# Moving a difference and a three-way split to GpSimd in a two-layer transformer kernel

## The chip, the cores and the metric

The kernel runs on one core of a Trainium2 chip. The metric is the device time of one execution in microseconds (us). Engines are named as in the profile: PE is the matrix engine, DVE is VectorE, ACT is ScalarE, POOL is GpSimd, and SP issues the DMAs. Each engine runs its own queue in order, and engines wait for each other by semaphores.

## The reference

Four sequences of 2048 tokens with 256 channels pass through two layers. Layer 0 is a causal attention with one head of 64 and a linear layer on fp8-rounded activations. Layer 1 is a causal attention with 16 heads of 16 and rotary positions, and a gated FFN that mixes each token with the one before it. Each of the four parts is added to its input behind a layer normalization without weights.

```python
x = x + attn0(layernorm(x))
x = x + ffn0(layernorm(x))
x = x + attn1(layernorm(x))
# FFN of layer 1, on h = layernorm(x); h_prev is h shifted by one token
xr = mu_r * h + (1.0 - mu_r) * h_prev
xk = mu_k * h + (1.0 - mu_k) * h_prev
x = x + sigmoid(xr @ W_r.T) * (square(relu(xk @ W_k.T)) @ W_v.T)
```

## The kernel before

**Tiles and stages.** The work goes in blocks of 512 tokens (`BLK`), 16 in all, ordered by sequence. Layer 1's attention is the main stream: for each block four groups of four heads, 64 groups in all, and for each group one step per 128 keys (4, 8, 12 or 16 steps, more for later blocks of a sequence). In a step PE computes the scores of four heads, transposed (`scores_of`, L799), ACT takes their exponential (L826), and PE weights the values with the exponentials of the step before (`weighted`, L841). In the same step PE computes scores for a later group, not transposed (`maxima_of`, L773), of which DVE only takes the maximum over the keys (L796). Four heads share PE by rows of 32.

**The maxima and their split.** When the last maximum of a group is taken, the function `end` inside `all_maxima` (L972) reduces them to one negative maximum per token and head, `nm` (L975, 128 partitions by 16 columns). `shift_pads` (L442) splits `nm` into three bfloat16 parts whose sum has its precision, by four small instructions (L445 to L448), each of which reads what the one before it wrote: the first part is `nm` rounded, `rest` is what is left, the second part is `rest` rounded, the third what is then left. The parts go into a zeroed tile `pad`. `shift_rows` (L450) has PE turn this tile (L455) and ACT copy the result into `sh` (L459). In the following group, matmuls of `ones` with `sh` add the shift to the scores. The call of `shift_of` (L1222) stands at the end of a group's last step, and `end` is called one step earlier for most groups. PE runs in order, so whatever stands behind L455 in its queue waits with it. Layer 0's attention (`a_mid`, L513) makes the same split for its one head, 16 times (L535).

**The side work and the order.** Everything else is written as generators: layer 0 (`a_in`, `a_mid`, `a_out`), the projections, rotation, keys and queries of layer 1 (`b_...`), and layer 1's output projection and FFN (`end_half`, L869, one for each half block of 256 tokens, 32 in all). They fill the gaps of the main stream. A planner decides while the program is written: the class `Clock` (L41) follows every instruction with a fixed price for each engine and form, and keeps when each buffer is written. A generator yields the PE work that its next piece takes, the number of buffers it needs, and the tiles it needs. The planner (`pull`, L1049) writes the piece when by its model these tiles are ready within 150 ns of PE's time. So a changed price or engine moves all later side work. The order in each engine's queue is that of writing.

**The mix.** In `end_half` the normalized tokens stand transposed in `xs_`, with one column more for the token before; `cur` is the view without that column. Small POOL copies (L889 to L893) fill the first column and keep the last one. For each of the two mixes and each half of the channels (128 on the partitions), ACT makes (1 - mu) * previous (L901), and DVE adds mu * current (L904). The factor 1 - mu is made once, in `prepare` (L315). The matmuls with `wk` (L914) and `wr` read the mixes.

Of the kernel before, what the change touches and what calls it, by code (L numbers as in the profile page):

```python
# [12 lines left out]
F32 = mybir.dt.float32  # L13
# [9 lines left out]
P = 128  # L23
# [167 lines left out]
def seq_kernel(  # L191
# [101 lines left out]
    wv = load_w(wvT, "wv", C)  # L293
    mu_sb = const.tile([P, 2, CK], F32, name="mu_sb")
    nc.sync.dma_start(mu_sb, mu)
    omu_sb = const.tile([P, 2, CK], F32, name="omu_sb")

    def prepare():

        wcf, wce, wcm = wfs
        nc.vector.tensor_scalar(wcf, wcf, 448.0, -448.0, ALU.min, ALU.max)
        nc.vector.tensor_scalar(
            wce.bitcast(I32), wcf.bitcast(I32), 0x7F800000, None, ALU.bitwise_and
        )
        nc.vector.tensor_scalar(wcm, wce, 2.0**-6, 1.5 * 2.0**20, ALU.max, ALU.mult)
        nc.vector.tensor_tensor(wcf, wcf, wcm, ALU.add)
        nc.vector.tensor_tensor(
            wf16.rearrange("p k n -> p (k n)"), wcf, wcm, ALU.subtract  # L310
        )
        nc.vector.tensor_scalar_mul(nsin_sb, sin_sb, -1.0)
        wv_flat = wv.rearrange("p k n -> p (k n)")
        nc.vector.tensor_scalar_mul(wv_flat, wv_flat, 0.5)
        nc.vector.tensor_scalar(omu_sb, mu_sb, -1.0, 1.0, ALU.mult, ALU.add)  # L315

# [57 lines left out]
    def w2t(name):  # L376
        return w2(name).rearrange("p (k n) -> p k n", k=CK)
# [61 lines left out]
        transpose(xn, out_to[0], f"{tag}_{hf}", nc.scalar.copy)  # L439
        done(1)  # L440

    def shift_pads(nm, pad, heads):  # L442
        part = [pad[:, :, :heads, i] for i in range(3)]
        rest = small.tile([P, TT, HG], F32, tag="rest", name="rest")[:, :, :heads]
        nc.vector.tensor_copy(part[0], nm)  # L445
        nc.vector.tensor_tensor(rest, nm, part[0], ALU.subtract)
        nc.vector.tensor_copy(part[1], rest)
        nc.vector.tensor_tensor(part[2], rest, part[1], ALU.subtract)  # L448

    def shift_rows(pad, sh, name):  # L450

# [61 lines left out]
    def a_mid(b, qb):  # L513
        tag = f"a0_{b}_{qb}"
        while (b, qb, "in", 0) not in flags or (b, qb, "in", 1) not in flags:
            yield None
        qh, ql = q0.pop((b, qb))[:2]

        mx = small.tile([P, TT, NB], F32, tag="mx0", name=f"mx_{tag}")
        for t in range(TT):  # L520
            for kb in range(qb + 1):
                yield 0.6, 0, qh, ql, kT0[kb]
                sc = bank(f"m_{tag}_{t}_{kb}")
                w = BLK if kb < qb else (t + 1) * P
                for q in (qh, ql):
                    nc.tensor.matmul(  # L526
                        sc[:, :w], q[:, t * P : (t + 1) * P], kT0[kb][:, :w],
                        start=(q is qh), stop=(kb < qb and q is ql),
                    )
                if kb == qb:  # L530
                    nc.tensor.matmul(sc[:, w - P : w], ident_b, mask_b, start=False, stop=True)
                nc.vector.reduce_max(mx[:, t, kb : kb + 1], sc[:, :w], axis=AX.X)  # L532
        nm = small.tile([P, TT], F32, tag="nm0", name=f"nm_{tag}")
        nc.vector.tensor_reduce(nm, mx[:, :, : qb + 1], AX.X, ALU.max, negate=True)
        shift_pads(nm[:, :, None], pads[2], 1)  # L535
        yield 0.3, 2, pads[2][:, :, 0, :3]
        sh = work.tile([P, BLK], BF16, tag="sh0", name=f"sh_{tag}", bufs=2)
        shift_rows(pads[2], sh, f"sh_{tag}")
        cx, sums = w2(f"cx_{tag}"), w2(f"sum_{tag}")

        nkt = (qb + 1) * TT
        pTs = []
        for kt in range(nkt):
            yield 0.9, 1, sh
            sc = bank(f"s_{tag}_{kt}")
            pT = w2(f"p_{tag}_{kt}")
            c0 = max(kt - qb * TT, 0) * P
            keys = kT0[kt // TT][:, (kt % TT) * P : (kt % TT + 1) * P]
            diag = kt >= qb * TT
            nc.tensor.matmul(sc[:, c0:], ones, sh[:, c0:], start=True, stop=False)  # L550
            nc.tensor.matmul(sc[:, c0:], keys, qh[:, c0:], start=False, stop=False)
            nc.tensor.matmul(sc[:, c0:], keys, ql[:, c0:], start=False, stop=not diag)
            if diag:
                nc.tensor.matmul(
                    sc[:, c0 : c0 + P], ident_b, maskT_b, start=False, stop=True
                )
            nc.scalar.activation(pT[:, c0:], sc[:, c0:], AF.Exp, scale=D0**-0.5)  # L557
            pTs.append(pT)
            if kt % 2:
                if diag:  # L560
                    c0 -= P
                    nc.gpsimd.memset(pT[:, c0 : c0 + P], 0.0)
                narrow.append((b, qb, kt - 1, c0, pTs, cx, sums))
                pTs = []
        done(2)
        while (b, qb, "ctx", nkt - 2) not in flags:
            yield None
        ctx0[b, qb] = cx, sums
# [300 lines left out]
    def end_half(b, qb, x, cn, hf):  # L869
        tag = f"f1_{b}_{qb}_{hf}"  # L870
        yield 0.6, 2, cn[:, 2 * hf : 2 * hf + 2, :]
        cT = w2t(f"cT_{tag}")
        transpose(cn[:, 2 * hf : 2 * hf + 2, :], cT, f"c{tag}", nc.scalar.copy)
        flags.add((b, qb, "cT", hf))
        yield 1.8, 0, cT
        po = bank(f"po_{tag}")
        for j in range(2):
            token_mm(po[:, j * C : (j + 1) * C], cT, wo1, j)
        done(1)
        xh = x[:, 2 * hf : 2 * hf + 2, :].rearrange("p t c -> p (t c)")  # L880
        nc.vector.tensor_tensor(xh, po, xh, ALU.add)

        xs_ = work.tile([P, CK, HALF + 1], F32, tag="xs", name=f"xs_{tag}", bufs=2)
        cur = xs_[:, :, 1:]
        yield from normal_T(x, [cur], hf, f"f1_{b}_{qb}")
        while hf and (b, qb, 0) not in edges:
            yield None
        if (qb, hf) == (0, 0):
            nc.gpsimd.memset(xs_[:, :, 0:1], 0.0)  # L889
        else:  # L890
            nc.gpsimd.tensor_copy(xs_[:, :, 0:1], edges.pop((b, qb - (1 - hf), 1 - hf)))
        edges[b, qb, hf] = small.tile([P, CK, 1], F32, tag="edge", name=f"edge_{tag}", bufs=3)
        nc.gpsimd.tensor_copy(edges[b, qb, hf], xs_[:, :, HALF : HALF + 1])  # L893
        while hf and (b, qb, "mid") not in flags:
            yield None
        yield 0.0, 3, xs_
        mix = []
        for i in (1, 0):
            m = w2t(f"mix_{tag}_{i}")
            for k in range(CK):  # L900
                nc.scalar.activation(  # L901
                    m[:, k, :], xs_[:, k, :HALF], AF.Copy, scale=omu_sb[:, i, k : k + 1]
                )
                nc.vector.scalar_tensor_tensor(  # L904
                    m[:, k, :], cur[:, k, :], mu_sb[:, i, k : k + 1], m[:, k, :],
                    ALU.mult, ALU.add,
                )
            mix.append(m)
        xk, xr = mix
        yield 1.8, 0, xk  # L910
        pk = bank(f"pk_{tag}")
        for d in range(CK):
            for k in range(CK):
                nc.tensor.matmul(  # L914
                    pk[:, d * HALF : (d + 1) * HALF], wk[:, k, d * P : (d + 1) * P],
                    xk[:, k, :], start=(k == 0), stop=(k == CK - 1),
                )
        done(1)
        ka = w2(f"ka_{tag}")
        nc.scalar.activation(ka, pk, AF.Relu)  # L920
        nc.gpsimd.tensor_tensor(ka, ka, ka, ALU.mult)
        flags.add((b, qb, "mid"))
        yield 1.8, 0, xr
        pr = bank(f"pr_{tag}")
        for j in range(2):
            token_mm(pr[:, j * C : (j + 1) * C], xr, wr, j)
        done(1)
        sg = w2(f"sg_{tag}")

        nc.scalar.activation(sg, pr, AF.Tanh, scale=0.5)  # L930
        yield 1.8, 0, ka
        po = bank(f"pw_{tag}")
        for j in range(2):
            token_mm(po[:, j * C : (j + 1) * C], ka.rearrange("p (k n) -> p k n", k=CK), wv, j)
        nc.vector.scalar_tensor_tensor(sg, sg, 1.0, po, ALU.add, ALU.mult)  # L935
        nc.gpsimd.tensor_tensor(xh, xh, sg, ALU.add)  # L936
        done(2)
        t0 = qb * BLK + hf * HALF
        nc.sync.dma_start(
            out[b, t0 : t0 + HALF, :].rearrange("(t p) c -> p t c", p=P),  # L940
            x[:, 2 * hf : 2 * hf + 2, :],
        )
        flags.add((b, qb, "end", hf))
# [16 lines left out]
    def all_maxima():  # L960


        for G, (i, b, qb, g) in enumerate(groups):
            n = steps[G]
            lead = steps[max(G - 1, 0)]
            for s in range(n):
# [5 lines left out]
                def end(G=G, s=s, n=n, mx=mx, qb=qb, b=b, g=g):  # L972
                    if s == n - 1:
# [1 line left out]
                        nc.vector.tensor_reduce(  # L975
                            nm, mx[:, :, :, : qb + 1], AX.X, ALU.max, negate=True
                        )
                        shift_pads(nm, pads[G % 2], HG)

                yield at_, i, (b, qb, g, s, mx), end  # L980

# [331 lines left out]
```

## Time and profile before

| | |
|---|---|
| time before, median of 3 runs | 3005.61 us (2993.38 to 3006.42) |
| profiled execution | 2996.61 us |
| its span | 2994.9 us |
| granted PE clock, mean | 0.97 |
| PE idle between matmuls in the span (2994.9 - 2813.5) | 181 us |
| L901, ACT's part of the mix | 128 instructions, mean 505 ns |
| L904, DVE's part of the mix | 128 instructions, mean 557 ns |
| L445 / L446 / L447 / L448, the split | 64 / 64 / 80 / 80 instructions (L447 and L448 with the 16 of layer 0), mean 267 / 228 / 229 / 232 ns |
| two-input POOL instructions, 256 and 512 columns (L692, L936) | mean 736 and 1294 ns |

The profile is that of one execution. Its first part gives each engine's busy time as a share of the span; its chain follows the work that ended last back through whatever released each step. A group of instructions is shown as line, engine, operation, tiles and count, then busy time, mean duration in ns, and the idle time of the engine just before them with what ended it. An engine that stands idle costs nothing unless the chain runs over it.

### The profile page before, as it was taken

Reading aid. Unit: us, or ns where it says so; the run is one execution under the profiler, and the core shown is the slowest. Engines: PE = TensorE matmul, PEld = TensorE weight load, DVE = VectorE, ACT = ScalarE, POOL = GpSimd, SP = SyncE. Lnnn points to the kernel's source line nnn. Section 1 sums busy time; section 2 is a strip of 40 time slices with the busy share of each in tenths; the row PEclk is TensorE's granted clock in tenths of the full one; section 3 lists DMA queues with packets and bytes.
Section 4 is the critical chain, followed back from the end, with each engine's and each line's share of the span. In section 5 each row is a group of like instructions: output and inputs, shape, how many; then the busy total and the mean of one; then the engine's idle time right before and its main releaser. Section 6 shows DMA issues by size and latency. Waiting matters only on the chain.

```text
span 2994.9 us, 68331 instructions
## 1 busy us (share of the span) xinstructions
PE 2813.5 (94%) x27616; PEld 1532.4 (51%) x27616; DVE 2095.7 (70%) x4536; ACT 1743.4 (58%) x3681; POOL 913.8 (31%) x1246
## 2 busy tenths in 40 slices
PE   6899999999999999999999999999999999999998
PEld 3555555555456555545455555554545655454444
DVE  4567767787566787887747677878765678678761
ACT  2445467566654656656665565666666555665664
POOL 4524344041232405313214342513122341340001
PEclk9889999999999999999999999999999999999999
DMA  2000000000000000000000000000000000000000
GB/s 89 1 12 5 22 2 5 23 1 26 4 9 15 5 22 5 22 2 5 23 12 5 12 16 12 5 23 2 26 2 12 16 5 15 2 8 2 5 2 11
DMA packets 28781, 36.70 MB, mean 12 GB/s; under 512 B 3312, under 2 KB 22064, under 8 KB 28464
## 3 DMA queue, kind: packets, MB, share of 16 engines
q1 hardware_dynamic: 28464, 32.32, 3.8%
q8 instruction: 217, 3.56, 0.5%
q14 instruction: 100, 0.82, 0.1%
HBM read 11.24 MB, written 8.39 MB: 7 GB/s over the span
## 4 chain that ended last, share of the span: by engine, by line
PE 74%; DVE 18%; ACT 3%; POOL 2%; issue 2%; DMA 1%; POOLq 0%; SPq 0%; DVEq 0%; ACTq 0%
PE av L844 16%; PE s L811 14%; PE m L781 13%; DVE mx L796 10%; PE pq_a L423 3%; PE pv_a L423 2%; PE pk_f L914 2%; PE av_a L580 2%; PE pr_f L423 2%; PE po_f L423 2%; PE pw_f L423 2%; ACT p L826 1%; DVE mx_a L532 1%; PE m L790 1%; PE s_a L550 1%
## 5 line engine op out<-in xcount | busy, mean ns | idle before, releaser
L796 DVE TENSOR_REDUCE mx<-m 128x1 f32<-128x512 f32 (+3 forms) x2560 | 1414.3, 602 | 524.8 <-PE m L781 222.6
L826 ACT ACTIVATE p<-s 128x512 f32<-128x512 f32 (+3 forms) x2560 | 1223.5, 533 | 852.9 <-PE s L811 467.7
L781 PE MATMUL m<-kT_a,qh_a 32*128 32x512 f32 (+3 forms) x2560 | 698.8, 463 | 66.2 <-DVE mx L796 47.2
L811 PE MATMUL s<-qh_a,kT_a 32*128 32x512 f32 (+3 forms) x2560 | 651.3, 502 | 8.0 <-ACT p L826 4.2
L844 PE MATMUL av<-p,v_a 128*32 128x512 f32 (+3 forms) x5120 | 644.0, 548 | 0.1
L781 PEld LDWEIGHTS m<-kT_a,qh_a 32*128 32x128 f32 x2560 | 297.9, 186 | 598.7 <-DVE mx L796 223.1
L781 PE MATMUL m<-kT_a,ql_a 32*128 32x512 f32 (+3 forms) x2560 | 535.8, 390 | 0.0
L811 PE MATMUL s<-sh,ones 32*128 32x512 bf16 (+3 forms) x2560 | 483.7, 356 | 18.2 <-ACT p L826 13.7
L811 PE MATMUL s<-ql_a,kT_a 32*128 32x512 f32 (+3 forms) x2560 | 482.7, 367 | 0.0
L781 PEld LDWEIGHTS m<-kT_a,ql_a 32*128 32x128 f32 x2560 | 261.0, 189 | 20.8 <-issue 19.5
L811 PEld LDWEIGHTS s<-qh_a,kT_a 32*128 32x128 f32 x2560 | 250.9, 189 | 33.3 <-ACT p L826 10.2
L811 PEld LDWEIGHTS s<-ql_a,kT_a 32*128 32x128 f32 x2560 | 250.0, 188 | 1.2
L811 PEld LDWEIGHTS <-ones 32*128 32x128 bf16 x2560 | 126.6, 91 | 184.7 <-issue 161.1
L844 PEld LDWEIGHTS av<-p,v_a 128*32 128x32 f32 x5120 | 112.0, 108 | 161.5 <-issue 117.0
L587 POOL TENSOR_TENSOR sum_a<-p_a,p_a 128x512 f32<-128x512 f32 x16 | 20.5, 1279 | 466.5 <-ACT p_a L557 441.6
L592 POOL TENSOR_TENSOR sum_a<-sum_a,p_a 128x512 f32<-128x512 f32 (+1 forms) x128 | 146.6, 1145 | 5.0
L819 PE MATMUL s<-mask_q,mask_k 32*128 32x128 bf16 (+1 forms) x2048 | 136.9, 208 | 0.0
L790 PE MATMUL m<-mask_k,mask_q 32*128 32x64 bf16 x2048 | 129.8, 197 | 0.0
L592 POOL TENSOR_TENSOR cx_a<-cx_a,avs_a 128x512 f32<-128x512 f32 (+1 forms) x64 | 73.1, 1143 | 180.3 <-ACT avs_a L590 180.3
L423 PE MATMUL pq_a<-wqkv,xT_a 128*128 128x512 f32 x256 | 123.5, 605 | 1.9 <-DVE mx L796 1.8
L936 POOL TENSOR_TENSOR x<-x,sg_f 128x512 f32<-128x512 f32 x32 | 41.4, 1294 | 271.4 <-DVE sg_f L935 271.4
L532 DVE TENSOR_REDUCE mx_a<-m_a 128x1 f32<-128x512 f32 (+3 forms) x160 | 87.5, 600 | 11.9 <-PE m_a L526 8.4
(163 smaller groups left out, 3991.2 us busy)
## 6 DMA issues: line engine op xcount, KB each, us to landing
x<-in_x SPq DMA_DIRECT2D x16, 512.0 KB, 4.0
out_y<-x SPq DMA_DIRECT2D x32, 256.0 KB, 2.1
qh_a<-th_a SPq DMA_DIRECT2D x32, 128.0 KB, 2.4
ql_a<-tl_a SPq DMA_DIRECT2D x32, 128.0 KB, 2.4
kT_a<-th_a SPq DMA_DIRECT2D x16, 128.0 KB, 2.4
kT_a<-tl_a SPq DMA_DIRECT2D x16, 128.0 KB, 2.4
wqkv<-in_wqkv1T SPq DMA_DIRECT2D x1, 768.0 KB, 8.6
wc<-in_wfT SPq DMA_DIRECT2D x1, 256.0 KB, 7.0
```

Of the source, the lines that this page charges most:

```text
L423: nc.tensor.matmul(dst, lhsT[:, k, t * P : (t + 1) * P], w[:, k, :], start=(k == 0), stop=(k == CK - 1),)
L532: nc.vector.reduce_max(mx[:, t, kb : kb + 1], sc[:, :w], axis=AX.X)
L580: nc.tensor.matmul(av[z * SLOT : (z + 1) * SLOT, c0:], v0[kt // TT][:, kt % TT + j, d * SLOT : (d + 1) * SLOT], pTs[j][:, c0:], start=True ...
L592: nc.gpsimd.tensor_tensor(to[:, c0:], to[:, c0:], add[:, c0:], ALU.add)
L781: nc.tensor.matmul(sc[:, :w], q1[b, qb, g // 2][i][r, g % 2, t * P : (t + 1) * P], kT1[b, kb][r, g, :w], start=(i == 0), stop=(kb < qb and ...
L790: nc.tensor.matmul(sc[:, w - P + lo : w - P // 2 + lo], mask_q[r, v, :], mask_k[r, v, lo : lo + P // 2], start=False, stop=(v == 1),)
L796: nc.vector.reduce_max(mx[:, t, h, kb : kb + 1], sc[:, :w], axis=AX.X)
L811: nc.tensor.matmul(sc[:, c0:], lhsT, rhs, start=(i == 0), stop=(i == 2 and not diag))
L819: nc.tensor.matmul(sc[:, c0 : c0 + hi], mask_k[r, v, :], mask_q[r, v, :hi], start=False, stop=(v == 1),)
L826: nc.scalar.activation(pTs[h][:, c0:], sc[:, c0:], AF.Exp, scale=DK**-0.5)
L844: nc.tensor.matmul(av[h * SLOT : (h + 1) * SLOT, c0:], v1[b, kt // TT][:, kt % TT, at : at + SLOT], pTs[h][:, c0:], start=(kt == 0), stop= ...
L914: nc.tensor.matmul(pk[:, d * HALF : (d + 1) * HALF], wk[:, k, d * P : (d + 1) * P], xk[:, k, :], start=(k == 0), stop=(k == CK - 1),)
```

## The change

The mix is written with one difference: previous + mu * (current - previous). POOL makes the difference once for each half block, DVE makes both mixes from it, and ACT has no part in it; the difference lies in the tile of the mix that is made last. The tile of 1 - mu is dropped. `shift_pads` takes the engine as an argument: POOL for the 64 groups of layer 1, DVE as before for layer 0.

```diff
-    omu_sb = const.tile([P, 2, CK], F32, name="omu_sb")
...
-        nc.vector.tensor_scalar(omu_sb, mu_sb, -1.0, 1.0, ALU.mult, ALU.add)
...
-    def shift_pads(nm, pad, heads):
+    def shift_pads(nm, pad, heads, engine):
         part = [pad[:, :, :heads, i] for i in range(3)]
         rest = small.tile([P, TT, HG], F32, tag="rest", name="rest")[:, :, :heads]
-        nc.vector.tensor_copy(part[0], nm)
-        nc.vector.tensor_tensor(rest, nm, part[0], ALU.subtract)
-        nc.vector.tensor_copy(part[1], rest)
-        nc.vector.tensor_tensor(part[2], rest, part[1], ALU.subtract)
+        engine.tensor_copy(part[0], nm)
+        engine.tensor_tensor(rest, nm, part[0], ALU.subtract)
+        engine.tensor_copy(part[1], rest)
+        engine.tensor_tensor(part[2], rest, part[1], ALU.subtract)
...
-        shift_pads(nm[:, :, None], pads[2], 1)
+        shift_pads(nm[:, :, None], pads[2], 1, nc.vector)
...
         yield 0.0, 3, xs_
-        mix = []
-        for i in (1, 0):
-            m = w2t(f"mix_{tag}_{i}")
+
+        mix = [w2t(f"mix_{tag}_{i}") for i in range(2)]
+        nc.gpsimd.tensor_tensor(mix[0], cur, xs_[:, :, :HALF], ALU.subtract)
+        yield 0.0, 0, mix[0]
+        for m, i in ((mix[1], 1), (mix[0], 0)):
             for k in range(CK):
-                nc.scalar.activation(
-                    m[:, k, :], xs_[:, k, :HALF], AF.Copy, scale=omu_sb[:, i, k : k + 1]
-                )
                 nc.vector.scalar_tensor_tensor(
-                    m[:, k, :], cur[:, k, :], mu_sb[:, i, k : k + 1], m[:, k, :],
+                    m[:, k, :], mix[0][:, k, :], mu_sb[:, i, k : k + 1], xs_[:, k, :HALF],
                     ALU.mult, ALU.add,
                 )
-            mix.append(m)
-        xk, xr = mix
+        xr, xk = mix
         yield 1.8, 0, xk
...
-                        shift_pads(nm, pads[G % 2], HG)
+                        shift_pads(nm, pads[G % 2], HG, nc.gpsimd)
```

## The prediction

> **What bounds the kernel now.** I read the page first: busy shares, the chain that ended last, and the groups of the lines that the diff touches. Each group line ends in busy time, mean ns of one instruction, and idle time before it with what ended it.
>
> ```profile
> PE 2813.5 (94%) x27616; PEld 1532.4 (51%) x27616; DVE 2095.7 (70%) x4536; ACT 1743.4 (58%) x3681; POOL 913.8 (31%) x1246
> ...
> PE 74%; DVE 18%; ACT 3%; POOL 2%; issue 2%; DMA 1%; POOLq 0%; SPq 0%; DVEq 0%; ACTq 0%
> ```
>
> PE is the bound; DVE is the second limit: 18% of the chain runs over it, most of it (10%) the maxima L796, whose reductions free the banks that PE needs. GpSimd (POOL) has room. Between its matmuls PE is idle for only 181 us, so an edit off the chain brings little. The groups concerned:
>
> ```profile
> L904 DVE SCALAR_TENSOR_TENSOR mix_f<-xs_f,mu_sb,mix_f 128x256 f32<-128x256 f32 x128 | 63.6, 557 | 28.5 <-ACT mix_f L901 28.5
> ...
> L901 ACT ACTIVATE mix_f<-xs_f,omu_sb 128x256 f32<-128x256 f32 x128 | 54.5, 505 | 0.0
> ...
> L455 PE MATMUL pt_sh<-ident_b,pad 128*128 128x128 bf16 x256 | 25.8, 224 | 18.5 <-DVE pad L448 16.1 <-ACT p L826 1.9
> ```
>
> Two things matter. DVE stands in its queue for 28.5 us, in 23 places, for ACT's half of the mix. And PE itself waits 16.1 us for the last part of the split, DVE pad L448: the split that is to be moved is on the path already. The timeline of one such place (start, duration, engine and line; in brackets the idle time and its releaser):
>
> ```profile
> 115.08 0.18 DVE L975 TENSOR_REDUCE nm<-mx 128x16 f32<-128x16 f32 x1
> 115.29 0.20 DVE L445 CAST pad<-nm 128x16 bf16<-128x16 f32 x1
> 115.53 0.18 DVE L446 TENSOR_TENSOR rest<-nm,pad 128x16 f32<-128x16 f32 x1
> 115.75 0.20 DVE L447 CAST pad<-rest 128x16 bf16<-128x16 f32 x1
> 115.98 0.23 DVE L448 TENSOR_TENSOR pad<-rest,pad 128x16 bf16<-128x16 f32 x1
> ...
> 116.27 0.61 PE L455 MATMUL pt_sh<-ident_b,pad 128*128 128x128 bf16 x4 [2.15 <-DVE pad L448]
> ```
>
> From the end of nm (115.26) to the last part (116.21) is 0.95 us; PE starts 0.06 later. I read the same lines at all 64 groups: in 30 the first L455 starts 0.06 us after L448, so the split is the last thing waited for; in the others PE comes 0.15 to 13.7 us later.
>
> **Part 1, the mix.** Per half block (32 of them) four ACT copies go, and one POOL subtraction 128x512 comes. The four DVE instructions stay, with the same shape and again two SBUF inputs. A mix in the timeline and in the chain (start, us, what):
>
> ```profile
> 2784.99 1.70 ACT L901 ACTIVATE mix_f<-xs_f,omu_sb 128x256 f32<-128x256 f32 x4
> ...
> 2785.54 1.68 DVE L904 SCALAR_TENSOR_TENSOR mix_f<-xs_f,mu_sb,mix_f 128x256 f32<-128x256 f32 x4 [0.48 <-ACT mix_f L901]
> ```
> ```profile
> 2785.11 1.59 ACT mix_f L901 x4
> 2786.70 0.49 ACT p L826
> ```
>
> ACT is held for 1.70 us and DVE for 0.48 + 1.68. Here the exponentials behind the mix are late and PE waits for one. Over the whole chain, walked piece by piece, ACT mix holds 28.6 us and DVE mix 25.0. After the change ACT's part is gone and DVE starts when the difference is there, without a wait of its own, since a new yield lets the planner take it up then. But DVE is still held for 1.68 us and is late next. So the gain per half lies between 0 (DVE's hold covers all of it) and 0.89 us (28.6 / 32). I take the wait that goes: the first ACT copy of 0.50 us plus 0.04 of handing over, 32 x 0.54 = **-17 us**. Bounds 0 and -29.
>
> The subtraction costs POOL 1.28 us (rows L936, L624: 1.26 to 1.29), 41 us in all. Elsewhere it stands in parallel to PE; cover gone, it shows in the tail. There PE's first L914 of the two last halves starts 1.2 us after the first ACT copy; with 0.08 hop + 1.28 + 0.48 + 0.40 + 0.06 it would start 2.3 us after it: 2 x 1.1 = **+2 us**. The dropped (1 - mu) preparation is one DVE instruction of 0.16 us at the start: nothing. No DMA is added, removed or moved.
>
> **Part 2, the split on POOL.** 64 x 4 small instructions move; the 16 single-head splits stay on DVE. POOL shows no such instruction at 16 columns. Nearest rows: copies of 2 columns 0.185 (L893), a tensor_scalar of 2 columns 0.22 (L397), two-input instructions 0.735 at 256 and 1.279 at 512 columns, whose line leads to 0.22 at 16. Dependent POOL instructions leave 0.08 us between them (L397 to L399, L683 to L688), and DVE to POOL takes 0.08 (L395 to L397). So 0.08 + 0.20 + 0.08 + 0.23 + 0.08 + 0.20 + 0.08 + 0.23 = 1.18 us against 0.95. Lower bound: as on DVE, no difference. Upper bound: a two-input instruction of 2 columns that takes 0.72 (L399, a power) for both subtractions, 2.2 us. I take 1.18, since copies, scalars and the line agree on it.
>
> POOL runs in order, so the split also waits for what POOL was given before it. I set, for each of the 64 groups, the end of the POOL work that stands before it against nm's end: POOL is free in 51. In thirteen it is busy, for 0.1 to 2.4 us more; eight of these have slack enough or little to wait for, but in groups 22, 38 and 54 two normalizations (L397, L399) hold it for 2.13 us and PE would be 1.33 us late, in 57 (2.37 us) 0.6. With each group's own slack: 30 x 0.23 + 3 x 1.33 + 0.6 = **+12 us** (+4 at DVE's price, +49 at the upper bound).
>
> Behind the split on POOL stand the copies for the next queries (L745), zeroings (L562) and edge copies (L891, L893), which now and then run up to 22 us ahead and will wait for nm. Their readers start 2.5 us or more after nm's end, but for one copy at 1.25: **+1 us**.
>
> What DVE gains: 64 x 0.87 = 56 us of its queue. In the 30 tight groups this time was PE's wait anyway. In the other 34, 30 us go; of the maxima's busy time 22% is on the chain (312 of 1414), so 30 x 0.22, some **-6 us**.
>
> [...]
>
> **Sum**: -17 + 2 + 12 + 1 - 6 = **-8 us**. The profiled execution took 2996.6 us (span 2994.9 and 1.7 around it), 9 below the median of the runs, 3005.6 (2993.4 to 3006.4). Carried to the median: **2998 us**; from the profiled execution it would be 2989. A measurement here tells about 0.5% (15 us) from no change.
>
> **Rivals.**
> - *ACT's queue was the limit* (faster). For it: many mixes are on the chain by ACT alone, such as that at 2785, and ACT loses 54.5 us. Against it: DVE's hold of equal length remains. Then -29 for the mix, and DVE's relief counts fully, 56 x 22% = -12; with +2, +12, +1: -26, **2980 us**.
> - *POOL's queue takes the place of DVE's* (slower). The place is the split in front of L455. POOL is busy 31% of the time, in runs of up to 4.2 us (the rotation, L683 to L692). My order is that of the old trace; the planner writes another with the new prices. If the split meets POOL at random, it waits 0.31 x 2.1 = 0.65 us on average, in 64 groups 42 us in place of 12. With the other terms as above: +22, **3028 us**. It decides from a mean delay of about 0.55 us per group on (35 us in all). Against it: POOL was free in 51 of 64.
> - *The wait for ACT becomes a wait for POOL* (no change). If the difference is later than the planner thinks, DVE stands in its queue again. Then 0 instead of -17: +9, **3015 us**, within the bound. Against it: its price for a POOL instruction of 512 columns is 1.28 us, as traced.
> - *Another order by itself*: all later work is placed by modelled times, so it shifts. The second and third batch, nearly the same work, take 721.6 and 720.2 us, nm to nm; over four batches such a difference is some 6 us either way, within the forecast.
>
> **Chances.** Forecast and the third rival, both within 0.5%: 0.41. ACT's queue: faster, 0.34. POOL's queue or dear POOL instructions: slower, 0.25. The range goes from 2972 (the first rival and some of the order) to 3030 (the second).
>
> **What would show it.** Right: L901 gone, DVE's idle before the mix far below 28.5 us, a POOL split of 1.1 to 1.3 us, PE's wait for the pad near 16.1 + 12 us, now released by POOL. Wrong on the faster side: that wait not grown, and ACT p's share of the chain (1.4%) smaller. Wrong on the slower side: PE's wait for POOL pads over 45 us, or DVE waiting on POOL's difference. If POOL's small subtractions take 0.7 us, the price was wrong, not the mechanism.

## The result, and the profile after

The changed kernel takes **2967.11 us** (median of 4 runs, 2961.88 to 2970.98) against 3004.4 us for the kernel before (4 runs): a ratio of 0.988, 95% interval [0.985, 0.991], some 35 us faster. The forecast was 2998 us, the range 2972 to 3030: the time lies 5 us below the range. The profiled execution took 2966.1 us (span 2964.4 us, granted clock 0.971; before 0.970).

The page of the changed kernel, the same two lines as before and the first line of the split:

```profile
PE 2789.2 (94%) x27616; PEld 1525.5 (51%) x27616; DVE 2025.5 (68%) x4279; ACT 1698.3 (57%) x3553; POOL 1011.0 (34%) x1534
...
PE 73%; DVE 17%; POOL 5%; issue 3%; ACT 2%; DMA 1%; SPq 0%; POOLq 0%; ACTq 0%; DVEq 0%
...
L443 POOL CAST pad<-nm 128x16 bf16<-128x16 f32 x64 | 17.0, 266 | 384.2 <-DVE nm L971 352.7
```

DVE lost 70 us of busy time, ACT 45, POOL gained 97. PE runs as many matmuls, but is busy for 24 us less, and idle for 175 us where it was 181. So in the profile the larger part of the gain is not a wait that went. Keep that in mind: nothing in the sum of the prediction touches PE's busy time.

The waits of PE, changed kernel (who waits, for what, total us, times, longest us):

```profile
PE m L779 <- DVE mx L794: 54.8, 163, 0.6
PE pt_sh L453 <- POOL pad L446: 32.3, 35, 2.5
...
PE s L809 <- DVE mx L794: 3.6, 8, 1.4
...
PE s L809 <- ACT p L824: 0.5, 3, 0.2
```

and the same rows of the kernel before (its line numbers are 2 higher):

```profile
PE m L781 <- DVE mx L796: 47.2, 142, 0.6
...
PE s L811 <- ACT p L826: 17.9, 26, 0.9
PE pt_sh L455 <- DVE pad L448: 16.1, 20, 2.1
```

Two rows moved most. PE's scores hardly wait for exponentials any more (17.9 to 0.5 us), and PE waits 16.2 us more for the split, which POOL now releases. They nearly cancel. The wait for maxima also grew, by 7.6 us. One split on POOL, in the timeline (start, duration, in brackets idle time and releaser):

```profile
114.42 0.18 DVE L971 TENSOR_REDUCE nm<-mx 128x16 f32<-128x16 f32 x1
...
114.67 0.25 POOL L443 CAST pad<-nm 128x16 bf16<-128x16 f32 x1 [5.78 <-DVE nm L971]
115.00 0.23 POOL L444 TENSOR_TENSOR rest<-nm,pad 128x16 f32<-128x16 f32 x1
115.29 0.25 POOL L445 CAST pad<-rest 128x16 bf16<-128x16 f32 x1
115.62 0.27 POOL L446 TENSOR_TENSOR pad<-rest,pad 128x16 bf16<-128x16 f32 x1
...
115.95 0.61 PE L453 MATMUL pt_sh<-ident_b,pad 128*128 128x128 bf16 x4 [2.48 <-POOL pad L446]
```

From the end of nm (114.60) to the end of the last part (115.89) it takes 1.29 us, forecast 1.18. And the mix: DVE waits for POOL's difference in one place only (before, for ACT's copies, 28.5 us in 23 places).

```profile
L901 DVE SCALAR_TENSOR_TENSOR mix_f<-mix_f,mu_sb,xs_f 128x256 f32<-128x256 f32 x128 | 59.6, 528 | 2.9 <-POOL mix_f L897 2.9
```

### The profile page after: what moved, and what is told of

Read it like the earlier page. It is cut to its first block, busy times and chain, and to the rows that moved or that the text cites. A ratio compares the mean times of both kernels' runs of the same rounds, so it can differ in the third digit from the quotient of the medians.

```text
span 2964.4 us, 68254 instructions
## 1 busy us (share of the span) xinstructions
PE 2789.2 (94%) x27616; PEld 1525.5 (51%) x27616; DVE 2025.5 (68%) x4279; ACT 1698.3 (57%) x3553; POOL 1011.0 (34%) x1534
## 4 chain that ended last, share of the span: by engine, by line
PE 73%; DVE 17%; POOL 5%; issue 3%; ACT 2%; DMA 1%; SPq 0%; POOLq 0%; ACTq 0%; DVEq 0%
PE av L842 16%; PE s L809 13%; PE m L779 13%; DVE mx L794 11%; PE pq_a L421 3%; PE pv_a L421 2%; PE m_a L524 2%; PE av_a L578 2%; PE pk_f L910 2%; PE po_f L421 2%; PE pr_f L421 1%; PE pw_f L421 1%; PE m L788 1%; PE pq_a L484 1%; PE s_a L548 1%
## 5 line engine op out<-in xcount | busy, mean ns | idle before, releaser
L809 PE MATMUL s<-sh,ones 32*128 32x512 bf16 (+3 forms) x2560 | 476.7, 356 | 4.3 <-DVE mx L794 3.6
L809 PEld LDWEIGHTS s<-qh_a,kT_a 32*128 32x128 f32 x2560 | 249.9, 188 | 25.2 <-issue 11.8
L443 POOL CAST pad<-nm 128x16 bf16<-128x16 f32 x64 | 17.0, 266 | 384.2 <-DVE nm L971 352.7
L817 PE MATMUL s<-mask_q,mask_k 32*128 32x64 bf16 (+1 forms) x2048 | 136.6, 208 | 0.0
L917 POOL TENSOR_TENSOR ka_f<-ka_f 128x512 f32<-128x512 f32 x32 | 33.3, 1041 | 224.2 <-ACT ka_f L916 224.2
```

What stands on the lines that cost most here:

```text
L809: nc.tensor.matmul(sc[:, c0:], lhsT, rhs, start=(i == 0), stop=(i == 2 and not diag))
L817: nc.tensor.matmul(sc[:, c0 : c0 + hi], mask_k[r, v, :], mask_q[r, v, :hi], start=False, stop=(v == 1),)
```

## The experiments

The planner makes another order of the side work from the new prices, so the change is two things at once: new work, and a new order. To part them, the planner's clock was given two functions: `aside()` does not price what was just written, and `price()` prices something else in its place. With the old prices for new work PE's queue keeps the order of the kernel before, and the reverse.

In the table, "us by ratio" is (ratio - 1) x 3000. The last column is span x mean granted clock, the median of the runs: what the span would be if PE never lost clock, and all else followed PE. It is a figure worked out, not measured; the kernel before gives 2904 to 2908 us on the four chips that were used. Each ratio is to the kernel before on the same chip, so kernels that ran on different chips are compared by their ratios. "Order" is that of PE's queue; in the traces it agrees with the order that a row names, but for matmuls that start at nearly the same moment. In e3 and g2 the difference stands a little earlier in POOL's queue than in the change and has a tile of its own.

| kernel | work | order | ratio [95%] | us by ratio | clock | span x clock |
|---|---|---|---|---|---|---|
| before | old | old | 1 | 0 | 0.970 | 2906 |
| change, f0 | new | new | 0.9887 [0.9862, 0.9911] | -34 | 0.971 | 2875 |
| e3 | new | old | 0.9965 [0.9954, 0.9975] | -10 | 0.971 | 2897 |
| e4 | old | new | 1.0015 [0.9999, 1.0032] | +5 | 0.969 | 2904 |
| g2 | new mix, old split | old | 0.9926 [0.9910, 0.9942] | -22 | 0.974 | 2895 |
| g3 | old mix, new split | old | 1.0043 [1.0027, 1.0060] | +13 | 0.964 | 2907 |
| f1 | new mix, old split | new | 0.9923 [0.9903, 0.9943] | -23 | 0.970 | 2880 |
| f2 | old mix, new split | new | 0.9957 [0.9942, 0.9972] | -13 | 0.975 | 2908 |
| f3 | as f2, ACT's copies earlier | new | 0.9957 [0.9936, 0.9978] | -13 | 0.973 | 2900 |
| g1 | change and idle ACT copies | new | 0.9935 [0.9914, 0.9956] | -20 | 0.972 | 2893 |
| e1 | new mix, old split | its own | 0.9970 [0.9954, 0.9987] | -9 | 0.968 | 2892 |
| e2 | old mix, new split | its own, near the old | 1.0033 [1.0020, 1.0046] | +10 | 0.968 | 2906 |
| g4 | old | gate 1400 | 1.0183 [1.0163, 1.0203] | +55 | 0.954 | 2912 |
| h1 | new | gate 1400 | 1.0007 [0.9996, 1.0018] | +2 | 0.965 | 2888 |
| h2 | old | BASE 1.70 | 1.0046 [1.0027, 1.0065] | +14 | 0.967 | 2906 |
| h3 | new | BASE 1.70 | 0.9977 [0.9964, 0.9989] | -7 | 0.972 | 2901 |
| h4 | old | BASE 1.80 | 0.9992 [0.9981, 1.0003] | -2 | 0.970 | 2904 |
| i1 | change, 3 waits filled | new | 0.9858 [0.9814, 0.9902] | -43 | 0.976 | 2882 |
| i2 | change, 29 waits filled | new | 0.9826 [0.9785, 0.9867] | -52 | 0.978 | 2879 |

**One part alone, with the order that it brings.** e1 is the change with the split left on DVE, e2 the kernel before with the split on POOL.

```diff
# e1, against the change (e2 is the reverse edit on the kernel before)
-                        shift_pads(nm, pads[G % 2], HG, nc.gpsimd)
+                        shift_pads(nm, pads[G % 2], HG, nc.vector)
```

> The mix from one difference, the split left on DVE, the planner free to place the work anew. Theory A (ACT's queue was the limit: the copies that go are what the time came from, and the split on POOL costs 12 us): ratio to before 0.985 to 0.990, faster than the whole change. Theory B (the split moved off DVE brings it): ratio 0.993 to 1.000. Theory C (a luckier order of the side work brings it): anything, since this kernel has an order of its own; no use for C by itself.

> The split on POOL, the mix as before. The prediction's own sum for this part is +12 +1 -6 = +7 us, ratio 1.002. Theory A: 1.000 to 1.005, and PE's wait for the pad grows from 16 us to 28 to 35 us. Theory B: 0.988 to 0.994.

Measured: 2989.37 us against 2998.1 (-9), and 3007.25 us (+10). Together that makes +1, and the change makes -34: the parts do not add up, so the order had to be held.

**New work in the old order, old work in the new order.**

```diff
# e3, against the change (also: the split is priced as on DVE)
+        xd = work.tile([P, CK, HALF], F32, tag="xd", name=f"xd_{tag}", bufs=2)
+        clock.follow()
+        nc.gpsimd.tensor_tensor(xd, cur, xs_[:, :, :HALF], ALU.subtract)
+        clock.aside()
...
+                clock.aside()
+                clock.price(
+                    "InstActivation", "act", [xs_[:, k, :HALF], omu_sb[:, i, k : k + 1]],
+                    [m[:, k, :]],
+                )
```

> All instructions of the change, but the planner is shown the old instructions with their old prices, so that PE's queue holds the same instructions in the same order as before; the difference is written right behind the edge copies and has a tile of its own. Theory A: ratio 0.986 to 0.992, nearly the whole gain. Theory C: 0.996 to 1.002, the change's work without its order brings what the prediction's sum said (-8 us) or less.

```diff
# e4, against before (also: the split is priced as on POOL, and written on DVE)
+        clock.price("InstTensorTensor", "pool", [cur, xs_[:, :, :HALF]], [mix[0]])
+        yield 0.0, 0, mix[0]
```

> The instructions of before, ACT's copies and DVE's split included, but the planner is shown those of the change, so that PE's queue has the order of the change. Theory A: ratio 0.996 to 1.004. Theory C: 0.985 to 0.991, most of the gain without any of the work saved.

Measured: 2987.96 us (-10) and 3000.82 us (+5). The new work in the old order brings what the sum of the prediction said (-8). The new order by itself brings nothing. Both together bring -34.

**Each part in each order.** f0 is the changed kernel once more, on the chip of f1 to f3. f1 keeps the order of the change and leaves the split on DVE; f2 keeps it and makes the mix in the old way; f3 is f2 with the ACT copies one piece earlier, so that DVE does not stand for them in its queue.

```diff
# f3, against f2
-        clock.price("InstTensorTensor", "pool", [cur, xs_[:, :, :HALF]], [mix[0]])
-        yield 0.0, 0, mix[0]
...
                 nc.scalar.activation(
                     m[:, k, :], xs_[:, k, :HALF], AF.Copy, scale=omu_sb[:, i, k : k + 1]
                 )
+        clock.aside()
+        clock.price("InstTensorTensor", "pool", [cur, xs_[:, :, :HALF]], [mix[0]])
+        yield 0.0, 0, mix[0]
```

> The changed kernel itself, unaltered, beside the next three on one chip. All theories: ratio to before 0.987 to 0.991.

> The change with the split back on DVE, the planner still shown the split on POOL, so that PE and ACT keep the order of the change. If the split on POOL costs here what it cost alone (PE's longer wait for the pad, 10 to 16 us): ratio 0.983 to 0.987, faster than the change. Theory B (the split's move carries the gain): 0.992 to 1.000.

> The change with the mix of before (ACT's copies directly ahead of DVE's instructions), in the order of the change, the split on POOL. Theory A (the new order pays only where DVE need not wait for ACT): ratio 1.000 to 1.007, the old mix gives all of the gain away. Theory C (the order alone carries the gain): 0.986 to 0.992.

> As the kernel before it, but ACT's four copies stand one piece earlier, where the change has its difference, so that ACT does the same work and DVE finds it done. If DVE's wait for ACT in its own queue is what costs: ratio 0.987 to 0.993, most of the gain back. If ACT's time as such costs (54 us of copies in front of the exponentials): as the kernel before it, 1.000 to 1.007.

Measured: 2963.53, 2974.81, 2984.75 and 2983.37 us against 2996.66 for the kernel before. In the new order the mix is worth -21 us (f2 to f0) to -28 (e4 to f1), and the split, +10 (e2) in an order near the old one, is worth -11 (f1 to f0) to -18 (e4 to f2). f2 and f3 lie between the ranges of both theories that were set against each other, so neither holds as it was put. PE's waits in f2:

```profile
PE pt_sh L465 <- POOL pad L458: 30.7, 33, 2.5
...
PE s L821 <- DVE mx L806: 15.3, 10, 4.0
PE s L821 <- ACT p L836: 12.3, 22, 1.0
```

Against the change, 11.7 us more for maxima and 11.8 more for exponentials. Where the 4.0 us come from is seen in e4, which has the same order (timeline):

```profile
1358.34 1.70 ACT L921 ACTIVATE mix_f<-xs_f,omu_sb 128x256 f32<-128x256 f32 x4
...
1358.89 3.50 DVE L924 SCALAR_TENSOR_TENSOR mix_f<-xs_f,mu_sb,mix_f 128x256 f32<-128x256 f32 x4 [3.49 <-ACT mix_f L921]
...
1364.10 0.58 PE L828 MATMUL s<-sh,ones 32*128 32x512 bf16 x1 [3.95 <-DVE mx L813]
```

DVE stood 3.49 us for ACT's copies, then its four instructions took 3.50 us while POOL did its rotation (L700 to L709, 0.73 to 1.32 us each), and the maxima behind them were late for PE. f3 takes this wait away, but the wait for exponentials stays, and the time is that of f2:

```profile
PE s L821 <- ACT p L836: 14.4, 20, 1.3
...
PE s L821 <- DVE mx L806: 3.4, 7, 1.4
```

So it is not DVE's standing in its queue that costs most. What is left is ACT's time, which the next run tests.

**ACT's time alone, and each part in the old order.** g1 is the change with four ACT copies for each half into a tile that nobody reads. g2 and g3 make one part of the change each, in the old order.

```diff
# g1, against the change
+        clock.follow()
+        spare = work.tile([P, CK, HALF], F32, tag="spare", name=f"spare_{tag}", bufs=2)
+        for i in (1, 0):
+            for k in range(CK):
+                nc.scalar.activation(
+                    spare[:, k, :], xs_[:, k, :HALF], AF.Copy, scale=mu_sb[:, i, k : k + 1]
+                )
+        clock.aside()
```

> The change as it is, with the four ACT copies of each half block put back ahead of DVE's mix, into a tile that nobody reads; the planner does not see them and all orders stay those of the change. If ACT's time in front of the exponentials is what the old mix costs in this order: ratio 0.993 to 0.997, most of the 21 us by which the old mix was slower. If DVE's wait for ACT and for its own second input is: 0.987 to 0.990, next to the change.

> The new mix alone, in the order of before on PE and DVE, the split on DVE. The prediction's sum for this part: -15 us, ratio 0.995. If the mix is worth the same in either order (about 25 us in the new one): 0.990 to 0.993.

> The split on POOL alone, in the order of before on PE and ACT. The prediction's sum for this part: +7 us, ratio 1.002; 1.001 to 1.005 if it costs what it cost with an order of its own (+10 us), 0.993 to 0.997 if it gains as in the order of the change (11 us).

Measured: 2980.56, 2978.48 and 3013.26 us against 3001.22. The idle copies alone take back 14 us of the 21 to 28 that the mix is worth in this order (0.9935 against 0.9887), and PE waits for exponentials again:

```profile
PE s L817 <- ACT p L832: 12.0, 21, 1.0
```

In g2, without the copies in the old order, that row falls from 17.9 us to:

```profile
PE s L819 <- ACT p L834: 2.4, 4, 0.7
```

So ACT's 128 copies in front of the exponentials are most of the mix's price in the new order. In the old order this row points the same way, but idle copies were not tried there.

In g3, the old order, the split can be held against the prediction group by group. It foresaw that PE would be 1.33 us later in groups 22, 38 and 54, and 0.6 later in 57: in the traces PE's idle time in front of the turned `pad` grows there by 1.29 us, three times, and by 0.63. In most of the others that grew it is 0.33 us (0.34 by the split's own times, 1.29 for 0.95). All 64 together go from 18.5 to 31.0 us, +12.5 for the +12 of the sum. But PE's waits for maxima hardly change (L781 and L811: 52.9 to 52.3 us), so the -6 us that DVE's relief was to bring do not show there, and the profile has 217.7 us at half clock where it was 179.6. So g3's +13 us are not the sum's +7 come true.

**Another order by itself.** One number of the planner that has nothing to do with the change is altered: the gate in `pull` that holds side work back while DVE is ahead, or BASE, a ceiling in the pacing of side work.

```diff
# g4 on before, h1 on the change
-                    if not asked[id(gen)][0] and clock.free["dve"] > clock.pe + (1500 if at[3] > TT else 2500):
+                    if not asked[id(gen)][0] and clock.free["dve"] > clock.pe + (1400 if at[3] > TT else 2400):
```
```diff
# h2 on before, h3 on the change (h4: 1.80 on before)
-    BASE = 1.75
+    BASE = 1.70
```

> The work of before, unaltered; in the planner one number differs (side work is held back when DVE's queue runs 1.4 or 2.4 us ahead of PE, not 1.5 or 2.5), which gives another order, as lawful as that of before. If orders differ by as much as the prediction held (6 us): ratio 0.997 to 1.003. If orders by themselves scatter by 20 us or more: outside of 0.995 to 1.005.

> The change with the planner's gate of g4 (1400 and 2400 ns for 1500 and 2500), which gives another order of the side work. If the order sets the time through the granted clock and the change's own gain is small beside it, this lies anywhere between 2960 and 3060 us, and its granted clock follows: span x clock stays between 2870 and 2900 us (before's work: 2895 to 2912) while the clock goes from 0.955 to 0.975. If instead the gain of 34 us belongs to the change's work in any order, it is 30 to 40 us faster than g4, 3015 to 3025 us.

> The kernel before with one number of the planner changed (BASE 1.70 for 1.75), work the same. If the order alone moves the time: a difference of 10 us or more from before, either way, with span x clock at 2906 +- 8 us. If order is worth some 6 us either way, as predicted: 2990 to 3012 us.

> The change with the same number changed (BASE 1.70). If the gain belongs to the work: 30 to 40 us faster than h2. If much of the 34 us is this one order's luck: a difference to h2 well outside that, with span x clock between 2870 and 2900 us, 10 to 30 us below before's.

> The kernel before with BASE 1.80 for 1.75, work the same. As h2: by the theory that the order moves the throttle, 10 us or more from before with span x clock at 2906 +- 8 us; by the predicted 6 us either way, 2990 to 3012 us.

Measured: 3054.52 us against 3001.22 (+55 by ratio), then 2996.76 (+2), 3006.8 (+14), 2989.16 (-7) and 2994.47 (-2) against 2995.36. The same work in five orders (before, e4, g4, h2, h4) spreads over 57 us. The change beats its partner in each of three pairs, by 34, 53 and 21 us. So neither side of the expectation holds in full: the change gains in each of these orders, but no fixed 34 us.

The last column of the table orders this. Nine kernels with the old mix, in any order, stand at 2900 to 2912 us, while their times go from 2983 to 3055: nearly all of that scatter is clock. The split on POOL changes this figure by -5 to +4 us in four pairings (before to g3, g2 to e3, f1 to f0, e4 to f2); by it, the +13 and -18 are the clock's too. Kernels with the new mix stand at 2875 to 2901 us, each below its partner with the old one: by 5 us (h2 to h3, the whole change) to 33 (f2 to f0, the mix alone).

**What takes the clock.** The trace has the granted clock, full or half (1.00 or 0.50), on a grid of 3.41 us. In the changed kernel it falls at the start of group 24, where PE stood 1.71 us for POOL's pad. That wait, then eight windows, cut 0.14 us ahead of the grid, which is why two of them show 0.52 and 0.98 (start:end, length, PE busy with its instructions, granted clock, DMA share, GB/s):

```profile
1076.72 0.61 PE L453 MATMUL pt_sh<-ident_b,pad 128*128 128x128 bf16 x4 [1.71 <-POOL pad L446]
```
```profile
1072.50:1075.91 3.41, 2.33 (x32) 1.00 0.30 79
1075.91:1079.33 3.42, 2.61 (x11) 0.52 0.44 151
1079.33:1082.74 3.41, 3.41 (x25) 0.50 0.50 116
1082.74:1086.15 3.41, 3.41 (x25) 0.50 0.49 115
1086.15:1089.57 3.42, 3.21 (x24) 0.50 0.02 5
1089.57:1092.98 3.41, 3.41 (x25) 0.50 0.00 0
1092.98:1096.40 3.42, 3.42 (x11) 0.50 0.00 0
1096.40:1099.80 3.40, 3.40 (x32) 0.98 0.00 0
```

PE was busy for 2.33 of 3.41 us, and then the clock was at half for six windows: 20.5 us, of which half, an estimate of 10 us, are lost. In groups 40 and 56 the same wait is followed by 13.7 us each. Is PE's idleness the cause? i1 fills a part of this one wait in the three groups with matmuls that nobody reads (0.83 us of the 1.71 are left in group 24), and leaves the order as it is; i2 does so in all 29 groups with a pad wait of 0.59 us or more.

```diff
# i1, against the change (i2: 29 groups, 4 to 21 matmuls)
+        clock.follow()
+        for t in range(idle):
+            nc.tensor.matmul(pt[:, :P], ident_b, ident_b, start=True, stop=True)
+        clock.aside()
         for t in range(TT):
...
+    IDLE = {24: 14, 40: 14, 56: 14}
```

> The change with 14 matmuls of 128x128 that nobody reads, put in front of the transposes of the shift in groups 24, 40 and 56, where PE stands 1.71 us for POOL's pad and where 20.5, 13.7 and 13.7 us at half clock follow in the profile. Everything else stays in its place. If the clock falls because PE was idle for much of a 3.4 us window, this filled wait leaves it at full speed there: 48 us at half clock go, worth some 24 us, so 2940 to 2950 us with a granted clock near 0.978. If the clock falls for another reason (heat, the kind of work, a fixed place), the half-clock stretch stays: 2962 to 2970 us.

> The same in all 29 groups where PE waits 0.59 us or more for POOL's pad in the profile of the change, with 4 to 21 such matmuls each, by the length of the wait. By the first theory the other places bring little more, since the waits there lie across two windows or are short: 2935 to 2955 us, and at worst some 0.1 us per group where the filling lasts longer than the wait. By the other, 2962 to 2975 us.

Measured: 2955.14 and 2945.37 us against 3001.8 for the kernel before. The grid windows of i1 at the same place:

```profile
1073.23:1076.65 3.42, 3.25 (x46) 1.00 0.22 77
1076.65:1080.06 3.41, 2.58 (x25) 1.00 0.47 153
1080.06:1083.47 3.41, 3.22 (x39) 1.00 0.79 183
```

The window is filled (3.25 us), and the clock stays at 1.00, even though the next window is no busier than before (2.58 us). Another place on the grid is not the reason: PE's wait ends 0.67 us behind a line of the grid in the change and 0.74 in i1. Group 24 as a whole, the change and then i1 (start:end, length, then busy us of PE, PEld, DVE, ACT and POOL, granted clock, DMA share, GB/s):

```profile
1076.60:1140.90 64.30, 63.22 (x543) 33.98 (x543) 43.23 (x85) 33.76 (x67) 11.93 (x16) 0.85 0.08 21
```
```profile
1077.40:1133.60 56.20, 54.98 (x543) 28.84 (x543) 42.61 (x85) 33.67 (x67) 11.91 (x16) 1.00 0.09 24
```

The same 543 matmuls, 8.1 us less. Groups 24, 40 and 56 together are 18.3 us shorter in i1 and in i2, and all 46 us at half clock in them are gone. So in these three groups PE's idleness is the cause, and the theory of another cause falls there. The whole of i1 lies in neither of its two ranges: it gains 8 us (12 against the first measurement of the change) for an expected 24, and its interval overlaps that of the change. Behind the filled places the work lies otherwise on the grid, and new stretches come elsewhere: a window at half clock each in groups 28 and 44, which had none in the change; all half-clock time of the profile falls from 173.5 to 151.4 us only. i2 lies in the expected range, and the profile has 108.6 us at half clock. Its 220 idle matmuls make it the fastest kernel of this study, 0.9826 [0.9785, 0.9867], against 0.9887 for the change. Its page:

```profile
PE 2776.1 (95%) x27836; PEld 1520.9 (52%) x27836; DVE 2024.0 (69%) x4279; ACT 1697.8 (58%) x3553; POOL 1011.0 (34%) x1534
```

More matmuls, and 13 us less busy time than in the change.

## Why the prediction was wrong, point by point

- **The failing step is the order, taken as a term by itself: "another order by itself ... some 6 us either way".** The mix and the split were priced in the order of the old trace, and a new order was only to add its 6 us. Measured, the same new work gives -10 us in the old order (e3) and -34 in its own (f0), while the new order with the old work gives +5 (e4). So 24 us come with the order and only together with the new work, and the price of a part depends on the order: the split costs +13 and +12 us in the old one (before to g3, g2 to e3) and gains 11 and 18 in the new (f1 to f0, e4 to f2); the mix gains 22 and 23 (before to g2, g3 to e3) and 21 and 28 (f2 to f0, e4 to f1).
- **Nor are the 6 us right for an order by itself.** Four other orders of the old work give -2, +5, +14 and +55 us. The estimate was read from two batches in one and the same order, and these could not show it: in the kernel before half-clock stretches of 13.7 us start at 916.1, 1636.3 and 2356.5 us, at the same place of each sequence, 720.2 us or 211 windows of the grid apart. Each batch repeated the other's luck.
- **The sum, -8 us, came out for what it described**, new work in the order of the old trace: -10 us (e3). That it came so near is partly luck: its parts measure -22 for -15 (g2) and +13 for +7 (g3), and the two misses cancel.
- **The mix was mis-sized: -17 and +2 forecast, -22 measured** in the old order (g2), -21 to -28 in the new. The forecast took the wait of DVE for the first copy as the gain. In the new order f3 and g1 show that most of it lies in ACT's queue: without the copies the exponentials come earlier. So the first rival had the mechanism of the mix right, and its 2980 us stand 13 us above the result; its price of -29 is about that of the new order. Of the two signs by which it was to be told, ACT p's share of the chain did fall (1.4% to 0.8%), and "that wait not grown" was wrong: the pad's wait did grow, and still the time fell. The price of POOL's difference, 1.28 us, was too high (1.056); the mix's instructions on DVE went from 557 to 528 ns in the mean.
- **The split's wait was right, its price was not.** 1.29 us on POOL for 1.18 forecast, PE's wait for the pad 32.3 us for 16.1 + 12, the small subtractions 0.24 and 0.27 us, and the late groups as foretold (g3). But in the order that the planner made the split gains 11 to 18 us where +7 was forecast. By span x clock it is worth -5 to +4 us in either order, so most of that swing would be the clock's.
- **"POOL's queue takes the place of DVE's"** did not come: PE's wait for pads is 32.3 us, below the 45 that it was to pass. **"The wait for ACT becomes a wait for POOL"** did not come either: 2.9 us in one place.
- **What stays open.** Why the new work gains so much more in its own order is not found. The mean clock of e3 and of the change are alike (0.971), so the 22 us of span x clock that lie between e3 and f0 are not half-clock time. In the profiles 7 us of PE's waits are part of them (168.7 and 161.7 us in all). Another 12 sit in PE's busy time, with half-clock time counted half (2719.7 and 2707.6 us), and were not traced to a place. Nor was it found why the new mix gains 24 to 33 us at full clock in the new order (e4 to f1, f2 to f0) and 10 to 11 in the old (g3 to e3, before to g2). So by times it is the split whose worth swings with the order, by span x clock it is the mix, and no run here decides between the two accounts. And the profiles and the other runs do not agree on each pair: in the profiles f0 has 183.6 us at half clock and f1 201.8, worth some 9 us, while the median clocks make it 3 us.

## What to carry to other kernels

Where a planner or a scheduler places work by prices, an edit of prices is an edit of the whole order: measure the new work in the old order and the old work in the new one before naming a cause, and try a harmless change of the planner to see how far order alone moves the time. Multiply the span by the mean granted clock before comparing two kernels: here some 70 us of scatter among kernels with the old mix came down to 12 us by that product. Where PE waits in an otherwise dense stretch (1.71 us in group 24 here), look at the clock behind the wait; filling such waits with matmuls that nobody reads paid here (i2: 0.9826 against 0.9887).

## What the runs showed of the hardware that was not expected

- **Short waits of PE were followed by half clock.** Over the 20 traces, on the 3.41 us grid: after a window at full clock in which PE was busy for less than 50%, the next was at half clock in 202 of 215 cases; at 50 to 70% in 136 of 296; at 70 to 90% in 149 of 2668; at 90 to 98% in 15 of 2799; above that in 0 of 10306. At half clock, the next window stayed there in 107 of 107 cases when PE was busy below 70%, in 283 of 329 at 70 to 98%, and in 145 of 600 above. The kernels are much alike, so these cases are not independent. None of the pad waits at groups 24, 40 and 56 was longer than 1.71 us, and the window ahead of group 24, cut as above, was 68% busy (2.33 of 3.41 us). PE's wait there was followed by 20.5 us at half clock, and with about half of it filled (0.83 us left, i1) the group was 8.1 us shorter. Waits of 1.74 us in groups 28 and 44 of the change, which lay otherwise on the grid, were followed by none, though a window there was 56 and 50% busy. So the busy share of one window did not decide by itself here.
- The runs of one kernel scatter with the granted clock. Beside i1 and i2 the kernel before ran in 2982.2 us at a mean clock of 0.976 and in 3006.38 at 0.965.
- POOL's subtraction L897, 128x512, of two views of one tile, took 1.056 us in the mean; the rows of two separate tiles that the forecast went by (L936, L624) had shown 1.28. That the tiles are the reason was not tested.
